# Writing the table of the first expert tiles three and four half steps later in a two-layer decoder

## Chip, core and metric

The kernel runs on one core of one Trainium2 chip. The metric is device time of one launch in microseconds (us): the median of several runs. Lower is better.

## Reference, cut to what matters

Sixteen sequences of 256 tokens with 128 features pass two decoder layers. Each layer normalises the tokens and adds, one after the other, self-attention, cross-attention to a short context, and a mixture of experts. The part that the change touches lies between layer 0's self-attention and its experts. All arithmetic is float32.

```
x = x + attn(ln(x))                       # 16 heads of 64, causal, linear bias
x = x + xattn(ln(x), ctx)                 # gate, 64 context tokens
xn = ln(x) * gamma + beta
probs = softmax(xn @ router_w); topv, topi = top_k(probs, 2)
comb = one_hot(topi) weighted by topv / sum(topv)
out = sum over e of comb[:, e] * ((silu(clip(gate_e)) * up_e) @ down_w[e])   # 8 experts
out = out + shared expert
x = x + out                               # then layer 1
```

## The kernel before, in words

**The stages.** Layer 0's self-attention goes over 16 sequences of 8 pairs of heads, 128 units. Eight chunks of 512 tokens (two sequences each) follow it: as soon as a chunk has left self-attention, its "front" (cross-attention, second normalisation, routing) is threaded between the units of later chunks. Then comes the expert stage: tokens lie in the DRAM tensor `rows_in`, sorted by expert, and 71 tiles of 128 rows (`NTILE`) are worked off one after the other; each reads its rows (`fetch`, L1315 to L1320), the gate and up weights of its expert (`weights`, L1326 to L1330) and multiplies (`hidden`, L1358 to L1369, and `down`, L1387). Layer 1 follows.

**Two tables.** Which expert a tile has, and where its rows start, is known only after the routing. The first 41 tiles (`EARLY`) are laid out as soon as six of the eight chunks are routed, so that the expert stage can start while chunks 6 and 7 are still to come; the other 30 tiles have a later table. The early table has two pieces, written in `early_pieces()`:

- the first: one matmul on TensorE that counts the routed tokens per expert (`mm_counts`, L921) and five VectorE operations on the counts (`tiles_of` and `starts_of`, L927 to L941);
- the second, `table2`: sixteen VectorE operations (`entries`, L950 to L976, then L987 to L992). L976 and L987 write `tab_a`, the row of expert numbers and the row of starting rows, that the queues read. L963 writes `etab`, used in the expert stage.

**What sets the order.** TensorE, VectorE, ScalarE and GpSimd follow a listed order in self-attention. A loop of 67 steps, two units (half steps) per step, walks the string `PLAN` and calls one piece of work per token: S scores, G the greatest of a row (L482), E exponentials (L494), R reciprocal (L502), N scaling on GpSimd (L508), T transposes (L524), C the copy of the transposes out of PSUM (L533), V the product with the values (L546), O its copy out (L556). Side pieces are entered in the dictionary `side` under a half step 2i or 2i+1; in step i, tokens m0 and m1 call their matmuls, and o0 and o1 what follows the matmul. In `PLAN`, o0 stands early and o1 late, after the last R. Each engine works strictly through its list; a piece that waits holds up all behind it on that engine.

**What the PSUM pool adds.** Transposes, the counts and the front's matmuls take turns in one PSUM pool of three buffers (`ps_m`): a transposition of a head pair needs two, and waits until an earlier user's copy has released them.

**The queues.** The expert weights (`gu`, 512 KB a tile) are issued by ScalarE between its own work, the first seven before the first expert tile; the rows (`xr`, 65 KB a tile) by SP, thirteen ahead. TensorE transposes a tile's rows (xTr, L1337), ScalarE copies them out (xTs, L1341), and the first product g (L1369) follows. Both wait for `tab_a`. SP's rows also wait for the last GpSimd scatter that fills `rows_in` (L830). Each DMA issued by ScalarE or SP signs off on one of eight DMA semaphores, shared by both and taken in turn. An issue waits until the DMA that had its semaphore before has landed, and what is behind it on the engine waits too.

Of the kernel before, what the change touches and what calls it, by code (L numbers as in the profile page):

```python
# [63 lines left out]
def kernel(ctx: ExitStack, tc: tile.TileContext, a: dict, out: bass.AP):  # L64
# [179 lines left out]
    with ExitStack() as ph:  # L244
# [669 lines left out]
        def new(what, shape):  # L914
            return fp.tile(list(shape), F32, tag=f"t_{what}", name=f"t_{what}")

        def mm_counts(tiles_seen):
            ps = tabled["ps"] = room["m"].tile(
                [P, E], F32, tag="m", name=f"counts_{tiles_seen}"
            )  # L920
            nc.tensor.matmul(ps, ones, seen[:, tiles_seen, :], start=True, stop=True)  # L921

        def tiles_of(what, less):


            cnt = new("cnt", (P, E))
            nc.vector.tensor_scalar(cnt, tabled.pop("ps"), -float(less), None, ALU.add)  # L927
            big = new("big", (P, E, T // P))
            nc.vector.tensor_tensor(
                big, cnt.unsqueeze(2).to_broadcast([P, E, T // P]), full, ALU.is_gt  # L930
            )
            num = tabled[what] = new(what, (P, E))
            nc.vector.tensor_reduce(num, big, AX.X, ALU.add)

        def starts_of(what, num):
            sq = new("sq", (P, E, E))
            nc.vector.tensor_tensor(
                sq, num.unsqueeze(1).to_broadcast([P, E, E]), lower, ALU.mult
            )
            start = tabled[what] = new(what, (P, E))  # L940
            nc.vector.tensor_reduce(start, sq, AX.X, ALU.add)  # L941

        def entries(tab, n, start, done):


            at = slice(0, EARLY) if done is None else slice(EARLY, NTILE)

            d = new("d", (1, E))
            if done is None:
                nc.vector.tensor_scalar(d, start[0:1, :], -float(P), None, ALU.mult)  # L950
            else:
                nc.vector.tensor_tensor(d, done[0:1, :], start[0:1, :], ALU.subtract)
                nc.vector.tensor_scalar(d, d, float(P), None, ALU.mult)
            dd = new("dd", (1, E))
            nc.vector.tensor_copy(dd[:, 0:1], d[:, 0:1])
            nc.vector.tensor_tensor(dd[:, 1:E], d[:, 1:E], d[:, 0 : E - 1], ALU.subtract)
            ge = new("ge", (P, EARLY, E))[:, 0:n, :]
            nc.vector.tensor_tensor(
                ge, tiles[:, 0:n, :], start.unsqueeze(1).to_broadcast([P, n, E]), ALU.is_ge
            )  # L960
            ex = new("ex", (P, EARLY))[:, 0:n]
            nc.vector.tensor_reduce(ex, ge, AX.X, ALU.add)
            nc.vector.tensor_scalar(etab[:, at], ex, -1.0, float(E + 1), ALU.mult, ALU.add)  # L963
            yield
            nc.vector.tensor_scalar(ex, ex, -1.0, None, ALU.add)
            ge, ex = ge[0:1], ex[0:1]
            nc.vector.tensor_tensor(
                ge, ge, dd.unsqueeze(1).to_broadcast([1, n, E]), ALU.mult
            )
            row = new("row", (1, EARLY))[:, 0:n]  # L970
            nc.vector.tensor_reduce(row, ge, AX.X, ALU.add)
            nc.vector.scalar_tensor_tensor(
                row, tiles[0:1, 0:n, 0], float(P), row, ALU.mult, ALU.add
            )
            nc.vector.scalar_tensor_tensor(row, ex, float(T), row, ALU.mult, ALU.add)
            nc.vector.tensor_copy(tab[:, 0, 0:n], ex)  # L976
            yield row

        def early_pieces():
            def table():  # L980
                tiles_of("num_a", P - 1)
                starts_of("start_a", tabled["num_a"])

            def table2():
                start = tabled["start_a"]
                row = list(entries(tab_a, EARLY, start, None))[-1]
                nc.vector.tensor_copy(tab_a[:, 1, :], row)  # L987

                done = tabled["done"] = new("done", (P, E))
                nc.vector.tensor_scalar(done, start, -1.0, float(EARLY), ALU.mult, ALU.add)  # L990
                nc.vector.tensor_scalar(done, done, 0.0, None, ALU.max)
                nc.vector.tensor_tensor(done, done, tabled["num_a"], ALU.min)  # L992

            return [(lambda: mm_counts(EARLY_C * TPC), table), (None, table2)]

        def late_pieces():
            def table():
                tiles_of("num_b", 0)
                left = new("left", (P, E))
                nc.vector.tensor_tensor(left, tabled["num_b"], tabled["done"], ALU.subtract)  # L1000
                starts_of("start_b", left)
                tabled["left"] = left

            def table2():
                tabled["rows"] = entries(tab_b, LATE, tabled["start_b"], tabled["done"])
                next(tabled["rows"])

            def table3():
                row = next(tabled["rows"])
                total = new("total2", (1, 1))  # L1010
                nc.vector.tensor_reduce(total, tabled["left"][0:1, :], AX.X, ALU.add)
                live = new("live", (1, LATE))
                nc.vector.tensor_scalar(live, tiles[0:1, 0:LATE, 0], total, None, ALU.is_lt)
                nc.vector.tensor_tensor(row, row, spare, ALU.subtract)
                nc.vector.tensor_tensor(row, row, live, ALU.mult)
                nc.vector.tensor_tensor(tab_b[:, 1, :], row, spare, ALU.add)

            return [(lambda: mm_counts(NT), table), (None, table2), (None, table3)]
# [8 lines left out]
        with tc.manual_schedule(engines=ordered | {mybir.EngineType.Pool}):  # L1027
# [51 lines left out]
            def plan(first, pieces):  # L1079
                for k, piece in enumerate(pieces):  # L1080
                    side.setdefault(first + k, []).append(piece)

            plan(17, [(lambda h=h: ctx_turn(h), lambda h=h: ctx_turned(h)) for h in range(2)])
            for c in range(NCHUNK):
                first_step = 16 * c + 22
                plan(first_step, front_pieces(c))
                if c == EARLY_C - 1:
                    plan(first_step + 24, early_pieces())
                if c == NCHUNK - 1:
                    plan(first_step + 25, late_pieces())  # L1090
            PLAN = (
# [35 lines left out]
            for i in range(steps // 2):  # L1127
# [13 lines left out]
                for tok, lag in plan_of:  # L1141
                    k = tok[0]
                    if k in "mo":
# [5 lines left out]
                        elif tok[1] in pieces:  # L1149
                            piece = pieces[tok[1]]  # L1150
# [405 lines left out]
    with ExitStack() as ph:  # L1556
# [230 lines left out]
        with tc.manual_schedule(engines=ordered):  # L1787
# [103 lines left out]
            plan = [w.split(":") for w in PLAN.split()]  # L1891
            plan = [(tok, int(lag)) for tok, lag in plan]
# [50 lines left out]
    with ExitStack() as ph:  # L1943
# [289 lines left out]
        plan = [part.split(":") for part in PLAN.split()]  # L2233
# [88 lines left out]
```

## Time and profile before

| | |
|---|---|
| median of 3 runs (lowest, highest) | 1412.21 us (1408.6, 1412.55) |
| the profiled execution | 1410.91 us, span 1409.0 us, mean granted TensorE clock 0.98 |
| busy share of the span: PE, DVE, ACT, POOL | 95%, 79%, 67%, 52% |
| layer 0 up to the first expert tile | 0 to 588 us: PE busy 568 us |
| expert stage | 588 to 818 us: PE busy 218 us |
| layer 1 | 818 to 1409 us: PE busy 555 us |

All further times are microseconds from the span's start. PE is TensorE's matmuls, DVE VectorE, ACT ScalarE, POOL GpSimd, SP the engine that issues most DMAs; ACTq and SPq are DMA issues. In a row of the timeline stand start, duration, engine, line, operation, output and inputs, count, and in brackets the idle time before and what ended it. The granted clock (PEclk) is a share of full speed.

### The profile page before, as it was taken

How to read it: one execution, taken by the hardware profiler on the slowest of the kernel's cores; microseconds unless marked ns; L12 is line 12 of the kernel's file. 1: busy time of each engine (PE TensorE's matmuls, PEld its weight loads, DVE VectorE, ACT ScalarE, POOL GpSimd, SP SyncE). 2: the span in 40 equal slices, each digit the busy share in tenths (PEclk: the TensorE clock that was granted, in tenths of full speed). 3: DMA queues.
4: the chain of work that ended last, by engine and by line, in shares of the span. 5: the costliest groups of instructions: out<-in, count | busy, mean ns of one | idle time of the engine just before them, and what ended most of it. 6: DMA issues, size and time to landing. Idle time of an engine off the chain costs nothing.

```text
span 1409.0 us, 37939 instructions
## 1 busy us (share of the span) xinstructions
PE 1342.1 (95%) x13205; PEld 1003.7 (71%) x13205; DVE 1108.8 (79%) x4483; ACT 942.6 (67%) x2532; POOL 733.7 (52%) x1153
## 2 busy tenths in 40 slices
PE   9999999999999999899899989999999987899998
PEld 7777777777777776689799966666666654566665
DVE  5776877777777778657779769999999977888874
ACT  6776767667676766344233349999999984776662
POOL 6463648475756656643433373553334315677751
PEclk9999999999999999999899999999999998999998
DMA  6772000000000000557577520000000000122122
GB/s 161 244 238 80 2 6 9 9 9 9 7 11 7 17 9 23 173 179 228 189 230 239 165 79 17 17 17 10 17 3 2 2 2 1 32 53 62 39 59 63
DMA packets 80349, 95.86 MB, mean 68 GB/s; under 512 B 19568, under 2 KB 62832, under 8 KB 80160
## 3 DMA queue, kind: packets, MB, share of 16 engines
q1 hardware_dynamic: 65328, 46.25, 12.0%
q10 hardware_dynamic: 10512, 38.28, 8.1%
q0 software_dynamic: 4320, 8.92, 1.9%
q8 instruction: 106, 1.74, 0.5%
q14 instruction: 83, 0.68, 0.2%
HBM read 64.24 MB, written 29.17 MB: 66 GB/s over the span
## 4 chain that ended last, share of the span: by engine, by line
PE 69%; ACT 17%; DVE 10%; issue 2%; POOL 1%; DMA 1%; POOLq 0%; ACTq 0%; SPq 0%; DVEq 0%
ACT p L1730 8%; PE pqk L414 8%; PE o L546 5%; PE s L469 5%; PE y L1387 5%; PE g L1369 5%; PE u L1369 5%; PE y L446 4%; PE t L524 4%; PE pv L431 3%; PE t L1748 3%; PE o L1772 2%; ACT pT L1759 2%; PE s L1708 2%; PE g L2149 2%
## 5 line engine op out<-in xcount | busy, mean ns | idle before, releaser
L508 POOL TENSOR_SCALAR p<-p,rs 128x128 f32<-128x128 f32 (+1 forms) x512 | 213.4, 431 | 166.3 <-DVE rs L502 124.4
L494 ACT ACTIVATE p<-p,nm 128x128 f32<-128x128 f32 (+1 forms) x512 | 226.4, 446 | 24.7 <-DVE nm L482 20.3
L1730 ACT ACTIVATE p<-p,nm 128x256 f32<-128x256 f32 x512 | 220.9, 508 | 1.7 <-DVE nm L1719 0.4
L1719 DVE CUSTOM_DVE_ANT_0 p<-s,strip 128x256 f32<-128x256 f32 x512 | 186.7, 419 | 15.3 <-PE s L1708 14.5
L533 DVE COPY pT<-t 128x384 f32<-128x384 f32 x256 | 130.2, 550 | 39.8 <-PE t L524 38.3
L482 DVE CUSTOM_DVE_ANT_0 p<-s,strip 128x128 f32<-128x128 f32 (+1 forms) x512 | 154.2, 348 | 0.5 <-PE s L469 0.2
L1397 POOL DMA_INDIRECT rows_out<-yr,to x71 | 68.5, 964 | 123.1 <-DVE yr L1396 116.3
L1748 PEld LDWEIGHTS t<-ident,p 64*128 64x128 f32 x2048 | 80.3, 140 | 54.5 <-issue 16.1
L546 PEld LDWEIGHTS o<-pT,v 128*64 128x64 f32 x1024 | 64.2, 138 | 66.4 <-issue 34.1
L425 ACT ACTIVATE k<-pqk 128x512 f32<-128x512 f32 x64 | 38.1, 596 | 108.3 <-PE pqk L414 108.3
L1748 PE MATMUL t<-ident,p 64*128 64x64 f32 x2048 | 102.9, 232 | 8.0 <-ACT pT L1759 2.4
L469 PE MATMUL s<-k,q 64*128 64x128 f32 (+1 forms) x1024 | 100.3, 332 | 0.3 <-DVE nm L482 0.3
L546 PE MATMUL o<-pT,v 128*64 128x256 f32 (+1 forms) x1024 | 99.0, 335 | 0.6 <-DVE pT L533 0.6
L1377 ACT ACTIVATE gs<-gs 128x512 f32<-128x512 f32 x71 | 44.7, 630 | 80.3 <-DVE gs L1376 62.3
L494 ACT ACTIVATION_READ_ACCUMULATOR p<-p,nm 128x1 f32 x512 | 98.0, 191 | 0.0
L524 PE MATMUL t<-ident,p 64*128 64x64 f32 x1536 | 81.6, 228 | 14.1 <-ACT pre L737 4.7
L524 PEld LDWEIGHTS t<-ident,p 64*128 64x128 f32 x1536 | 68.5, 139 | 35.7 <-POOL p L508 8.9
L1387 PE MATMUL y<-dn,hT 128*128 x568 | 79.3, 281 | 10.0 <-issue 10.0
L1708 PE MATMUL s<-k,q 32*128 32x256 f32 x1024 | 86.8, 410 | 1.4 <-DVE nm L1719 1.4
L1759 ACT COPY pT<-t 128x512 f32<-128x512 f32 x144 | 81.1, 588 | 6.8 <-PE t L1748 6.0
L440 DVE COPY v<-pv 128x512 f32<-128x512 f32 x64 | 44.2, 691 | 50.6 <-PE o L546 28.1
L1387 PEld LDWEIGHTS y<-dn,hT 128*128 128x128 f32 x568 | 71.3, 195 | 12.6 <-issue 11.8
(365 smaller groups left out, 3364.0 us busy)
## 6 DMA issues: line engine op xcount, KB each, us to landing
gu<-in_L_ffn_gate_up_w ACTq DMA_DIRECT2D x71, 512.0 KB
rows_in<-zero SPq DMA_DIRECT2D x131, 130.0 KB
spread<-wrows SPq DMA_DIRECT2D x16, 512.0 KB
xr<-rows_in SPq DMA_DIRECT2D x71, 65.0 KB
y<-rows_out SPq DMA_DIRECT2D x16, 256.0 KB
out_x<-yo SPq DMA_DIRECT2D x16, 128.0 KB
x<-in_x SPq DMA_DIRECT2D x7, 256.0 KB
rows_out<-yr,to POOLq DMA_INDIRECT x71
```

Source lines behind the costliest of these rows:

```text
L469: nc.tensor.matmul(ps_of[b, h][:, cols], q[rows, u2, iq], k[rows, u2, 0:nk], start=True, stop=True,)
L482: nc.vector.tensor_tensor_reduce(out=pr[:, cols], in0=ps[:, cols], in1=strip[:, h, P : 2 * P] if it == 0 else strip[:, h, :], scale=1.0, s ...
L494: nc.scalar.activation(pr[:, cols], pr[:, cols], AF.Exp, bias=nm[:, it : it + 1], scale=-1.0, accum_out=sm[:, it : it + 1],)
L508: nc.gpsimd.tensor_scalar(pr[:, cols], pr[:, cols], rs[:, it : it + 1], 1.0, ALU.mult, ALU.mult)
L524: nc.tensor.transpose(halves[r][:, i, blk, :], pr[rows, blk * P : (blk + 1) * P], ident[rows, rows],)
L533: nc.vector.tensor_copy(pT_of[u][:, :, :, r, :], tp_of[u][r])
L546: nc.tensor.matmul(po[rows, c0:N], v[:, jt, h % 8 * DH : (h % 8 + 1) * DH], pT[:, 0:N] if jt == 0 else pT[:, N:], start=(jt == 0), stop=(j ...
L1369: nc.tensor.matmul(ps[:, f, :], gu[:, lo + f * P : lo + (f + 1) * P], xT, start=True, stop=True,)
L1387: nc.tensor.matmul(ps, s["hT"][:, f, :], dn0[:, bass.ds(s["e"], 1), f, :].rearrange("p e d -> p (e d)"), start=(f == 0), stop=(f == NF0 - 1),)
L1719: nc.vector.tensor_tensor_reduce(out=pr[:, it, :], in0=ps[:, it, :], in1=strip1[:, h, (1 - it) * P : (1 - it) * P + N], scale=1.0, scalar= ...
L1730: nc.scalar.activation(pr[:, it, :], pr[:, it, :], AF.Exp, bias=nm[:, it : it + 1], scale=-1.0)
L1748: nc.tensor.transpose(halves[r][:, k, jt, it, :], pr[rows, it, jt * P : (jt + 1) * P], ident[rows, rows],)
```

## The change

The two pieces were planned for half steps 126 and 127 (`first_step` of chunk 5 is 102), the two halves of step 63. They go to half steps 129 and 131, the second halves of steps 64 and 65: the first piece three half steps later, the second four. No instruction is added or removed.

```
                 if c == EARLY_C - 1:
-                    plan(first_step + 24, early_pieces())
+                    for k, piece in zip((27, 29), early_pieces()):
+                        plan(first_step + k, [piece])
```

The order of the built program shows what this moves. On VectorE the five operations of the first piece stood between the pT copies (L533) of sequence 15's head pair 1 and the reciprocal L689; they now stand after the last G and R of head 13, ahead of the pT copies of pair 4. The sixteen of the second stood after the reciprocal of head 9, ahead of L701 and the pT copies of pair 2; they now stand after the last reciprocals (heads 14 and 15), ahead of L747 and the pT copies of pair 6. On TensorE the counting matmul moves from ahead of L431 to ahead of L721. On ScalarE the first seven weight issues move. They stood after the exponentials of heads 10 and 12, the copy L556 of pair 2, the exponentials of head 14, the copy of pair 4 (two issues) and the copy of pair 6. Now two stand after the copy of pair 4 and the other five after that of pair 6, all ahead of L1341, ScalarE's first work for an expert tile. SP keeps its order, but which DMA a semaphore belonged to before changes, since ScalarE's and SP's DMAs follow each other differently. GpSimd's order is the same.

## Prediction

> **What bounds the kernel.** The page first: PE is busy for 95% of the span, and the chain that ended last lies on it for 69%, DVE 10%. So a move pays where PE waits. Where it waits longest around the change is told by PE's waits between 540 and 605 us (us in total, times, longest):
>
> ```profile
> PE t L524 <- DVE rs L701: 4.2, 1, 4.2
> ```
>
> This one wait is the largest before the expert stage; the next there is 0.9. DVE's timeline tells what stood ahead of L701:
>
> ```profile
> 560.41 0.25 DVE L950 TENSOR_SCALAR t_d<-t_start_a 1x8 f32<-1x8 f32 x1
> ...
> 564.30 0.71 DVE L987 CAST tab_a<-t_row 1x41 int32<-1x41 f32 x1
> ...
> 565.63 0.17 DVE L701 RECIPROCAL rs<-sm 128x4 f32<-128x4 f32 x1
> ```
>
> The reader is to see the second piece, L950 to L992, hold DVE from 560.41 to L701's start: 5.2 us. PE had the PSUM buffer that L701 releases to wait for. Stretches of that time show what came after (us, then PE, PEld, DVE, ACT, POOL busy, granted clock, DMA):
>
> ```profile
> 561.80:565.90 4.10, 0.00 (x0) 0.00 (x0) 3.85 (x14) 0.73 (x4) 3.68 (x7) 0.91 0.10 32
> 566.00:572.00 6.00, 5.98 (x39) 4.41 (x40) 4.56 (x25) 2.56 (x9) 3.58 (x6) 0.50 0.67 197
> ```
>
> PE stood still, and then ran six microseconds at half clock. Last, ACT's timeline before the first expert tile:
>
> ```profile
> 579.92 4.16 ACTq L1330 DMA_DIRECT2D gu<-in_L_ffn_gate_up_w  x2
> 584.12 0.58 ACT L556 COPY oT<-o 128x512 f32<-128x512 f32 x1 [4.34 <-DMA xr<-rows_in]
> 584.86 0.36 ACTq L1330 DMA_DIRECT2D gu<-in_L_ffn_gate_up_w  x1
> 588.22 0.81 ACT L1341 ACTIVATE xTs<-xTr,bet,gam 128x128 f32<-128x128 f32 x2 [3.51 <-PE xTr L1337]
> ```
>
> Two weight issues spread over 4.16 us: the second waited until row tile 4 had landed, and the copy behind it waited too. xTs, on which the first expert product waits, starts at 588.22 because PE was late.
>
> **What goes.** The first piece held DVE from 556.29 (L927) to 557.79 (L689): 1.5 us that everything behind it on DVE and ACT saw. The second goes too; L701 then follows at about 559.1, when PE's sums (L695, 0.6 us after 558.5) are done. PE need no longer wait: transposes of pair 2 end at 559.5, scores (1.53) at 561.0, and pair 3's transposes start there, not at 565.95: 4.9 us earlier. If PE keeps its clock, they and their followers run at the times of undisturbed rows: 12 transposes 0.58 for 1.25, L708 0.66 for 1.12, L546 0.87 a pair for 2.77 in two; the L721 and L728 pairs 1.7 each. They end at 567.5 where they ended at 574.78. **Lead: 7.2 us.**
>
> **What comes back.** The first piece lies in DVE's idle 5.4 us before the pT copies of pair 4, which wait for ACT's two tanh (L737) anyway: nothing; without that cover 1.6 us. These copies end at 570.8 (before 578.2), two reciprocals at 571.0, and there the second piece now starts: 5.3 us in which the pT copies of pair 6, ready at 572.4, wait. Then L747 (0.67). Copies 576.9, pair 7's transposes 577.5 (they need a buffer that those copies free), last product 580.1, output product L446 (4.06) 584.2, its addition 584.6, xTr 585.1. Before, the second xTr ended at 588.2. **PE's side leads by 3.1.** But PE now idles from 572.4 to 577.5, 5.1 us, longer than the 4.18 that halved its clock. At half clock for the same 6.8 us, 3.4 us of PE work are lost less what waits anyway: about 2.7, xTr at 587.8. From nothing lost to 2.7: lead 3.1 or 0.4.
>
> **The new wait.** ACT and SP read the table when L987 is done: 4.6 us after the second piece's start, so 575.6 instead of 565.02. SP's first row issue was released by the last scatter then, at 575.80, long after the table; the scatters now land by 571 (last issue near 566.5, 3.8 us as before). The table now comes last, and SP needs 1.7 us from it to the issue (565.04 to 566.7 in its records): 577.3. Each further row tile takes 1.14 (thirteen table loads from 576.2 to 589.9), so row tile 7 is issued at 585.3. On ACT, weights 0 and 1 go out at 576 and 577, the copy of pair 6 at 580.1, weight 2 at 581.4. Counting each DMA semaphore's users in the built program, weight 3 waits for row tile 1, weight 4 for 3, **weight 5 for 6 and weight 6 for 7**; before, the last two waited for 4 and 6. xTs stands behind weight 6. Behind xTs stand the table load and the silu, and DVE, PE and the next tile wait for these.
>
> How long row tile 7 takes to land, the trace's packet records bound: of the first ten row tiles, from issue to the last receipt, tile 6 took 1.5 us, tile 8, issued amid weights, 4.0; the ten average 2.7, and tiles 7 and 9, also amid weights, took 3.5. Weights 1 to 4 are on the move here, so I take 3.1, between these two. Tile 7 lands at 588.4, weight 6 is out 0.4 later, and xTs starts at **588.9**; with 1.5 at 587.3, with 4.0 at 589.8. Weight 5 (tile 6: issued 584.1, landing 587.2, the next issue 1.1 after) asks for no more. PE's side, 585.1 or 587.8, is earlier. **Sum: 588.9 - 588.2 = +0.7 us**, with ends -0.9 and +1.6.
>
> In the expert stage the weights come later but not too late: seven tiles of 512 KB and thirteen of 65 KB from 577 on, at the 258 GB/s moved in 585 to 590, are there by 595; the seventh is wanted at about 609 (the first product of tile 6 started at 608.2). Cost nothing; at 139 GB/s (590 to 595) they would come at 610, and the cover is gone. PE is busy for 218 of that stage's 230 us, so a late start is carried to the end. Layer 1 has the same order and costs.
>
> [...] The row: 4.18 us idle, then 0.50 granted; waits of 0.6 us and less between 572 and 600 left it at 1.00. [...]
>
> **Rivals.**
> 1. **Slower: half clock at the first tiles.** Place: PE waits for xTs with xTr done. It decides from an idle between 0.6 us (kept) and 4.18 (halved); mine is 3.8 if the clock held before, 1.1 if not. Price: 6.8 us at half clock lose up to 3.4, less DVE and ACT waits in the first tiles (PE busy 4.8 to 5.0 of 5 there): 2 to 3.4. With the +0.7: +2.7 to +4.1, with the ends +1.6 to +5; 1414.5. For it: the idle is real in my sum. Against: the first idle probably takes the drop.
> 2. **Faster: the queues don't bite.** Row tiles land sooner than in 1.5 us of their issue, or SP issues them faster than every 1.14; then PE's side decides: -0.9 to -3.1, middle 1408.9. For it: 3.1 us of lead stand on PE. Against: ACT's 4.34 us wait of before is the same mechanism.
> 3. **Slower: weights late.** If the burst moves at 139 to 150 GB/s, tiles 3 to 6 wait 0.5 to 1 us each on top of rival 1: +4.3 to +8, 1417.
> 4. **Faster: the lead stays.** The second piece overlaps PE's products more than I think: -4.3 to -7.2 (the whole lead), 1405.
> 5. That the change doesn't do what it says: the listed order shows it does; no case of its own.
>
> **How the numbers follow.** The profiled execution took 1410.91, 1.91 around its span and 1.3 below the median 1412.21; I sum against it. Forecast 1410.91 + 0.7 = **1411.6**, its own range 1410.0 to 1412.5 (-0.9 to +1.6): 0.42. Rival 1 0.20, rival 2 0.16, rival 3 0.14, rival 4 0.08. About 0.3%, 4.2 us, is what a measurement of this kernel can tell from no change. Faster by more: rival 4 and a sliver of 2, 0.10. Slower by more: rival 3 and 0.06 of rival 1, 0.20. Same: 0.70. Leaving out rival 4 and the upper part of 3, the range goes from 1407.3 (-3.1, and 0.5 for the spread of the runs) to 1417.2 (+5, and 1.3 for profile against median).
>
> **What would show it.** Right: DVE's L950 begins near 571 with no PE wait on L701; PE idles some 5 us before pair 7's transposes; SP's first row issue at 577, right after the table; ACT's wait "DMA xr" stretching over weights 3 to 6, xTs near 589 with PE's xTr long done. Wrong: xTs right behind PE's xTr at 585 to 586 (rival 2), half clock after 589 (rival 1), first products waiting for gu (rival 3), or pT copies of pair 6 not held up (rival 4).

## Result and profile after

The changed kernel takes 1413.65 us (median of 22 runs, 1410.39 to 1417.18), the kernel before, run beside it as often, 1410.47 us (1406.51 to 1413.81). The ratio is 1.0026, 95% interval 1.0018 to 1.0035: **slower by about 3.7 us** (2.5 to 4.9). A second set (experiment 5) gave 1.0027 (1.0012 to 1.0041). The forecast was +0.7 us. The measured time lies inside its range and within the 0.3% that it called no change, but it is a real loss, five times the size of the one summed. The profiled execution took 1412.53 us with a span of 1410.7, so this one profile shows +1.6; single executions of either kernel scatter by 7 us, and the medians are the measure.

The waits of PE between 540 and 605 us, after (us in total, times, longest):

```profile
PE g L1370 <- DMA xr<-rows_in: 6.1, 1, 6.1
PE t L524 <- DVE pT L533: 4.0, 1, 4.0
PE t L524 <- POOL p L508: 1.4, 3, 1.0
```

The wait for L701 has gone, as forecast. Two others, 4.0 and 6.1 us, stand where one of 4.2 stood: the first is that for the pT copies of pair 6, the second ends at the first expert product. DVE's timeline shows the second piece at its new place (start, duration, engine, line, operation):

```profile
558.80 0.16 DVE L701 RECIPROCAL rs<-sm 128x4 f32<-128x4 f32 x1
...
570.08 0.41 DVE L950 TENSOR_SCALAR t_d<-t_start_a 1x8 f32<-1x8 f32 x1
...
573.65 1.98 DVE L975 SCALAR_TENSOR_TENSOR t_row<-t_ex,t_row 1x41 f32<-1x41 f32 x1
...
575.66 0.17 DVE L987 CAST tab_a<-t_row 1x41 int32<-1x41 f32 x1
...
576.84 1.02 DVE L533 COPY pT<-t 128x384 f32<-128x384 f32 x2
```

L701 runs at 558.80 and no longer at 565.63. The second piece holds DVE from 570.08, the table is written at 575.8, and the pT copies of pair 6 follow at 576.84. What ACT and PE did before the first expert tile, from their two timelines:

```profile
581.15 0.59 ACT L556 COPY oT<-o 128x512 f32<-128x512 f32 x1 [9.56 <-PE o L546]
581.87 9.76 ACTq L1331 DMA_DIRECT2D gu<-in_L_ffn_gate_up_w  x5
591.76 0.81 ACT L1342 ACTIVATE xTs<-xTr,bet,gam 128x128 f32<-128x128 f32 x2 [10.03 <-POOL vpad L1274]
```

```profile
585.76 0.44 PE L1338 MATMUL xTr<-ident,xr 128*128 128x128 f32 x2 [0.52 <-DVE x L454]
592.27 2.07 PE L1370 MATMUL g<-xTs,gu 128*128 128x128 f32 x8 [6.08 <-DMA xr<-rows_in]
```

Five weight issues spread over 9.76 us: they start at 581.87, 583.09, 584.21, 590.15 and 591.28, and the gap is weight 5 waiting for row tile 6. xTs stands behind them, at 591.76, with PE's xTr done since 586.2. (The releaser put to ACT's idle, POOL's vpad, ended at 591.59, but xTs doesn't read it: the two met by chance. In the second run of this kernel the same row names "DMA xr<-rows_in".) The same stretches as before, and three more (us, then PE, PEld, DVE, ACT, POOL busy, granted clock, DMA share, GB/s):

```profile
561.80:565.90 4.10, 3.80 (x24) 2.39 (x24) 3.85 (x23) 1.45 (x5) 3.74 (x6) 1.00 0.10 32
566.00:572.00 6.00, 3.72 (x46) 2.33 (x46) 3.90 (x12) 3.41 (x11) 5.76 (x9) 1.00 0.09 25
...
577.00:582.00 5.00, 4.55 (x32) 3.35 (x33) 3.31 (x9) 0.59 (x1) 0.00 (x0) 0.51 0.76 234
586.50:592.20 5.70, 0.00 (x0) 0.00 (x0) 0.00 (x0) 0.43 (x2) 5.09 (x9) 0.69 0.77 223
588.70:595.50 6.80, 3.23 (x15) 3.23 (x16) 1.08 (x4) 2.48 (x4) 2.89 (x9) 0.50 0.74 224
```

PE works where it stood still before (561.8 to 565.9) at full clock, but stands still from 586.5 to 592.2, and both new idles halve its clock: 0.51 after the first, 0.50 over the first two expert tiles.

### The profile page after: what moved, and what is told of

It is laid out like the page before. It is cut to its first block, busy times and chain, and to the rows that moved or that the text cites. A ratio compares the mean times of both kernels' runs of the same rounds, so it can differ in the third digit from the quotient of the medians.

```text
span 1410.7 us, 37935 instructions
## 1 busy us (share of the span) xinstructions
PE 1335.5 (95%) x13205; PEld 999.8 (71%) x13205; DVE 1109.3 (79%) x4483; ACT 943.3 (67%) x2532; POOL 735.9 (52%) x1153
## 4 chain that ended last, share of the span: by engine, by line
PE 68%; ACT 16%; DVE 10%; issue 2%; POOL 1%; DMA 1%; another core or an unknown queue 1%; SPq 1%; POOLq 0%; ACTq 0%; DVEq 0%
ACT p L1731 8%; PE pqk L414 8%; PE s L469 5%; PE o L546 5%; PE g L1370 4%; PE u L1370 4%; PE y L1388 4%; PE y L446 4%; PE t L524 4%; PE pv L431 3%; PE t L1749 3%; PE o L1773 2%; PE s L1709 2%; ACT pT L1760 2%; PE g L2150 2%
## 5 line engine op out<-in xcount | busy, mean ns | idle before, releaser
L508 POOL TENSOR_SCALAR p<-p,rs 128x128 f32<-128x128 f32 (+1 forms) x512 | 214.9, 435 | 161.1 <-DVE rs L502 119.6
L533 DVE COPY pT<-t 128x384 f32<-128x384 f32 x256 | 130.4, 550 | 36.9 <-PE t L524 35.1
L1370 PE MATMUL g<-xTs,gu 128*128 128x128 f32 x568 | 78.1, 282 | 14.3 <-ACT xTs L1342 8.1
L1370 PEld LDWEIGHTS g<-xTs,gu 128*128 128x128 f32 x568 | 71.4, 197 | 16.1 <-ACT xTs L1342 15.1
```

The lines of the kernel that those rows point to most:

```text
L508: nc.gpsimd.tensor_scalar(pr[:, cols], pr[:, cols], rs[:, it : it + 1], 1.0, ALU.mult, ALU.mult)
L533: nc.vector.tensor_copy(pT_of[u][:, :, :, r, :], tp_of[u][r])
L1370: nc.tensor.matmul(ps[:, f, :], gu[:, lo + f * P : lo + (f + 1) * P], xT, start=True, stop=True,)
```

## The experiments

**Theory:** the start of the expert stage is set by ACT's queue. Weights 5 and 6 wait for row tiles 6 and 7, these land late because weights are on the move at the same time, xTs stands behind the issues, and the half clock that follows PE's idle adds about 1 us. **Rivals:** the half clock, or weights and transfers that come late, are the loss; or DVE's hold of pair 6 is.

The sets ran on different chips: the kernel before took 1398.3, 1410.1 and 1399.4 us in the three sets below, so that times are compared as ratios to the kernel before in the same set. The changed kernel itself ran beside experiments 6 to 8, not beside 1 to 4, 9 and 10; for those its ratio is from another set. Up to the first expert tiles the profiles of all chips can be laid on each other to about a microsecond and a half: the transposes of pair 4 start at 567.26 and 567.41 in the changed kernel's two and at 566.72 in experiment 1, and xTr in experiment 2 starts 1.56 us ahead of the kernel before, whose stretch of half clock was longer (6.83 and not 3.41 us).

**1 and 2: xTs ahead of the late issues, in the changed kernel and in the one before.**

```
-            for i in range(AHEAD - 1):
+            for i in range(5):
                 weights(i)
...
                 if i < NTILE:
                     gated(i)
+                if i == 0:
+                    for j in range(5, AHEAD - 1):
+                        weights(j)
```

> The changed kernel with one more edit: before the expert stage only weights 0 to 4 are issued, and weights 5 and 6 behind the first tile's silu, so that the first xTs no longer stands behind the two issues that wait for row tiles 6 and 7. Theory A (ACT's queue behind the late row tiles sets the start of the expert stage): xTs starts right behind PE's xTr, near 586.5 instead of 591.8, PE's idle shrinks from 6.1 to about 1 us, no half clock at the first tiles, and the time is some 5 us below the changed kernel's, 1408 to 1410, that is 0.5 to 3.5 us below the kernel before. Theory B (the half clock and the late transfers of weights cost the time, the start of xTs does not): the first tiles wait for weights instead, and the time stays 2.5 to 4 us above the kernel before.

> The same edit of the weight issues in the kernel before. Theory A: there xTs waited for PE and not for ACT's queue, so nothing is to be had: within 0.7 us of the kernel before. If the edit by itself is worth several us (rival: late weight issues help the row tiles and the other traffic whatever the table does), it shows here too, and the first experiment says nothing about the changed kernel's loss.

Measured: 1.0004 (0.9984 to 1.0025) and 1.0008 (0.9992 to 1.0024) of the kernel before, medians 1399.56 and 1399.54 us. PE's timeline of the first:

```profile
586.75 1.13 PE L1370 MATMUL g<-xTs,gu 128*128 128x128 f32 x8 [0.58 <-DMA xr<-rows_in]
...
594.41 1.16 PE L1370 MATMUL g<-xTs,gu 128*128 128x128 f32 x8 [3.64 <-ACT xTs L1342]
```

and ACT's:

```profile
590.82 2.97 ACTq L1331 DMA_DIRECT2D gu<-in_L_ffn_gate_up_w  x3
593.90 0.46 ACT L1342 ACTIVATE xTs<-xTr,bet,gam 128x128 f32<-128x128 f32 x1 [4.63 <-DMA gu<-in_L_ffn_gate_up_w]
```

xTs starts at 586.18, right behind xTr, and the first products run at full clock (1.00 from 585 to 590): 5.6 us of theory A came as said. The time came back by 3, not 5 us, because the issues now hold up a later xTs: the products of the third tile wait 3.64 us. The kernel before pays for the edit in the same place (2.18 us there), within its uncertainty. What matters: **with xTs out of the queue on both sides, the move of the pieces costs nothing that can be told from zero** (medians 0.02 us apart; the scatter of the runs allows some 3 us either way, so this pair alone doesn't rule out most of the 3.7).

**3: PE kept busy in its second idle.**

```
+                if i == 0:
+                    spin = ps_m.tile([P, P], F32, tag="m", name="spin")
+                    for _ in range(22):
+                        nc.tensor.matmul(spin, ones, ones, start=True, stop=True)
                 if i < NTILE:
                     hidden(i)
```

> The changed kernel with 22 products of ones by ones on PE between the first xTr transposes and the first expert product, some 4.8 us that lie in PE's 6.1 us idle; nothing reads them. Theory A (the start counts most, the half clock adds about 1 us): xTs stays near 591.8, the clock stays at 1.00 behind it, and the time is 0.9 to 1.6 us below the changed kernel's, still 1.5 to 3 us above the kernel before. Theory B (the half clock is the loss): nearly all of the 3.5 us comes back. If the clock is not what the idle costs, nothing changes.

Measured: 1.0017 (1.0001 to 1.0034), against 1.0026 of the changed kernel: about 1.3 us less, though the intervals overlap. PE's first product and one stretch:

```profile
592.05 1.16 PE L1370 MATMUL g<-xTs,gu 128*128 128x128 f32 x8 [0.55 <-ACT xTs L1342]
```

```profile
590.00:595.00 5.00, 4.45 (x40) 4.26 (x39) 1.65 (x7) 2.72 (x4) 2.13 (x6) 1.00 0.73 229
```

xTs stays where it was (591.54), the clock holds at 1.00, the first product takes 1.16 and not 2.07 us. As far as overlapping intervals can tell, the half clock is a part of the loss, about a third or less, and the late start is the rest.

**4: only the second piece moved.**

```
-                    for k, piece in zip((27, 29), early_pieces()):
+                    for k, piece in zip((24, 29), early_pieces()):
```

> Only the second piece is moved (five steps later than in the kernel before), the first stays where the kernel before has it. By my steps the first piece holds DVE for 1.5 us ahead of L701 again, and the second starts and ends about 1.3 us later: table near 577, first row tile issued near 578.6, xTs near 593, 1 to 1.5 us above the changed kernel. Rival: the first piece costs nothing in either place, since the later DVE idle takes up what it delays: within 0.5 us of the changed kernel.

Measured: 1.0044 (1.0023 to 1.0064), some 2.5 us above the changed kernel. The first row issue came 1.35 us later (578.78), xTs 1.13 (592.89), as reckoned; xTr 2.1 (587.85):

```profile
593.40 2.07 PE L1370 MATMUL g<-xTs,gu 128*128 128x128 f32 x8 [5.12 <-ACT xTs L1342]
```

That the first piece's later place is worth its 1.5 us fits the profile; the interval (3.2 to 8.9 us above the kernel before) overlaps the changed kernel's and doesn't show it by itself.

**5 and 6: the changed kernel again, and with small weights.**

```
+            few = 256 if i in (2, 3, 4) else 2 * F0
             nc.scalar.dma_start(
-                gu, a["L0_ffn_gate_up_w"][bass.ds(e, 1)].rearrange("e d f -> d (e f)")
+                gu[:, 0:few],
+                a["L0_ffn_gate_up_w"][bass.ds(e, 1)].rearrange("e d f -> d (e f)")[:, 0:few],
             )
...
-                        ps[:, f, :], gu[:, lo + f * P : lo + (f + 1) * P], xT,
+                        ps[:, f, :], gu[:, at(lo + f * P) : at(lo + f * P) + P], xT,
```

Here `at` takes a column modulo 256 in tiles 2, 3 and 4, so that this kernel leaves out a part of the computation.

> The changed kernel itself once more, beside the others of this set and as often as they. [...]

> The changed kernel, in which weights 2, 3 and 4 fetch 256 of their 1024 columns (128 KB in place of 512) and the products of these three tiles read those columns four times over: that part of the computation is left out, the instructions of the engines are the same. The fewer packets also change which transfers share a completion semaphore: weight 5 now waits for row tile 3 and weight 6 for row tile 5. Theory A (row tiles are late because weights are on the move in the same engines, and ACT's queue hands that on): row tiles 5 to 7 land 2 to 3 us after their issue in place of 3.9 to 4.6, the last weight is issued near 586.5, xTs starts at 586.8 to 587.5 right behind xTr, there is no half clock behind it, and 4 to 5 us of the changed kernel's time go, to 0.5 to 2 us below the kernel before. Theory B (SP's own issues make row tiles late): rows 5 to 7 still take 4 us. Theory C (the start of the first tile is not what costs): the time stays.

Measured: 1.0027 (1.0012 to 1.0041) and **0.9990** (0.9979 to 1.0001): 5 us between them. In the traces a row tile's issue is followed by sixteen updates of its semaphore (tile 6 of the changed kernel: 588.89 to 590.13), and the issue that waits for it goes out behind the last (weight 5: 590.15); so the last is taken as the landing. From the traces' semaphore records, microseconds from a row tile's issue to that update:

```
row tile                      3     4     5     6     7
before                      2.75  3.34  2.38  1.82  3.85
changed                     2.59  3.57  5.14  5.87  4.94
changed, second run         3.06  4.14  4.51  3.86  4.81
small weights 2, 3 and 4    2.50  2.29  2.56  2.64  4.65
```

(The prediction counted completion packets over all DMA engines in order of time instead. That gives up to 1.3 us less in this table, 4.62 for tile 6 of the changed kernel, since a tile's updates are spread and late ones come behind early ones of the next: tile 7's first there came at 589.13, a microsecond ahead of tile 6's last.) With small weights on the move, row tiles 4 to 6 land in 2.3 to 2.6 us; tile 7, issued beside the next large weight, takes 4.65 again. SP issued all of them at the same moments as in the changed kernel (tile 6 at 584.26 in both), so theory B of this expectation is out. ACT and PE of the kernel with small weights:

```profile
581.88 4.74 ACTq L1332 DMA_DIRECT2D gu<-in_L_ffn_gate_up_w  x5
586.75 0.81 ACT L1344 ACTIVATE xTs<-xTr,bet,gam 128x128 f32<-128x128 f32 x2 [5.01 <-DMA gu<-in_L_ffn_gate_up_w]
```

```profile
587.26 1.16 PE L1372 MATMUL g<-xTs,gu 128*128 128x128 f32 x8 [0.97 <-ACT xTs L1344]
```

Five issues take 4.74 us and not 9.76, and xTs follows 5 us sooner. This run doesn't part the fewer bytes from the other partners on the semaphores: weights 5 and 6 have tiles 3 and 5 before them there, and tile 7, which landed only at 590.04, holds up nothing on ACT. That the queue hands the delay on is shown by the semaphores of the changed kernel (tile 6's last update at 590.13, weight 5 at 590.15) and by the first experiment's profile; that large weights on the move make the delay, by the table.

**7 and 8: the pieces in between.** The pairs are (26, 27); the eighth has the edit of the first as well.

```
-                    for k, piece in zip((27, 29), early_pieces()):
+                    for k, piece in zip((26, 27), early_pieces()):
```

> Both pieces between the kernel before and the changed one: the first at step +26, ahead of L715, the second at +27, right behind the reciprocals of head 13 and ahead of the pT copies of pair 4, where DVE idled for 3.6 us. Expected: second piece 565.7 to 571, no wait of PE for L701, pT copies of pair 4 held by about 3 us but those of pair 6 no longer; table ready near 570.5, first row tile issued near 572, row tile 7 landing by 584; xTr near 583, xTs at 584 to 586, 2 to 4 us ahead of the kernel before. Theory A: 1 to 4 us below the kernel before. Rival: a wait of the same length as the one before now stands ahead of pair 4, PE's clock is halved there as well, and the time is that of the kernel before within 1 us.

> The same places of the pieces, and weights 5 and 6 issued behind the first tile's silu. If ACT's queue still holds xTs at the new place, xTs comes up to 2 us earlier than without this edit and the time falls as much; if the row tiles are early enough, the edit only makes weights 5 and 6 late and costs 0.5 to 1.5 us, as it seems to in the kernel before.

Measured: **0.9989** (0.9979 to 1.0000) and 0.9992 (0.9983 to 1.0000): 1.1 to 1.6 us below the kernel before, at the edge of what can be told, and 5 us below the changed one. PE's waits in the seventh, and its ACT:

```profile
PE t L524 <- DVE pT L533: 4.9, 2, 4.4
PE g L1370 <- ACT xTs L1342: 1.0, 1, 1.0
```

```profile
577.32 2.78 ACTq L1331 DMA_DIRECT2D gu<-in_L_ffn_gate_up_w  x2
580.59 0.59 ACT L556 COPY oT<-o 128x512 f32<-128x512 f32 x1 [3.41 <-PE o L546]
581.44 4.17 ACTq L1331 DMA_DIRECT2D gu<-in_L_ffn_gate_up_w  x3
585.74 0.81 ACT L1342 ACTIVATE xTs<-xTr,bet,gam 128x128 f32<-128x128 f32 x2 [4.56 <-DMA gu<-in_L_ffn_gate_up_w]
```

PE still waits 4.4 us for DVE, about as long as before (4.2) and as in the changed kernel (4.0), and is halved behind it (0.53 granted from 573 to 578). But the table stands at 571.5, the row tiles are 4 us earlier, and xTs is ready within 0.5 us of xTr. So a DVE hold of this length doesn't decide; what is behind the table does. The edit of the first experiment adds nothing here, as expected once the rows are early.

**9 and 10: the second piece cut in two.** Its first six instructions go ahead of the pT copies of pair 4; the tenth has the edit of the first as well.

```
+            def table2a():
+                tabled["half"] = entries(tab_a, EARLY, tabled["start_a"], None)
+                next(tabled["half"])
+
-            def table2():
+            def table2b():
                 start = tabled["start_a"]
-                row = list(entries(tab_a, EARLY, start, None))[-1]
+                row = list(tabled.pop("half"))[-1]
...
-                    for k, piece in zip((27, 29), early_pieces()):
+                    for k, piece in zip((27, 27, 29), early_pieces()):
```

> The changed kernel with the second piece cut in two: its first six instructions (L950 to L963, 2.1 us) go to step +27 behind the first piece, into the 3.6 us that DVE idles ahead of the pT copies of pair 4, and only the rest (L965 to L992) stays at step +29. Expected: the rest runs from 570.1 to about 573, just as the pT copies of pair 6 become ready, so that PE's 4.0 us wait and the half clock behind it go; table near 572.7 (1.8 more if one of its operations is stretched again), first row tile issued near 574.3, xTr at 580 to 582. The completion semaphores are shared as in the changed kernel, so by theory A xTs still stands behind weights 5 and 6, which wait for row tiles 6 and 7: rows issued at 581.1 and 582.2 land by 585 to 586.5, xTs starts at 586.5 to 588.5, PE idles 5 us or more and may lose its clock: between 2.5 us below and 1 us above the kernel before. Rival (PE's own wait ahead of pair 7 was the loss): xTs follows xTr at 581 to 583 and 5 to 7 us are gained.

> The same cut, and weights 5 and 6 issued behind the first tile's silu. Theory A: xTs starts right behind xTr, at 580.5 to 582.5, 6 to 8 us ahead of the kernel before; some of it is lost at tile 3, where xTs waits behind the late weights (2 to 4 us, as in the two kernels before with this edit), so 2 to 6 us below the kernel before. Rival: the first tiles wait for their weights and row tiles instead, and it is no better than the kernel with the cut alone.

Measured: 1.0008 (0.9991 to 1.0025) and 0.9994 (0.9976 to 1.0011). The queue did what theory A says (xTs 587.90 with the issues ahead of it, 585.38 without), but PE's wait ahead of pair 7 only shrank to 3.3 us and xTr came at 585, not at 580 to 582: the rest of the piece took to 575.4. DVE and POOL of the ninth:

```profile
573.40 1.99 DVE L996 TENSOR_TENSOR t_done<-t_done,t_num_a 128x8 f32<-128x8 f32 x1
575.31 0.68 DVE L747 SCALAR_TENSOR_TENSOR xn<-pre,xn 128x512 f32<-128x512 f32 x1
```

```profile
574.11 1.25 POOL L750 TENSOR_TENSOR x<-x,pre 128x512 f32<-128x512 f32 x1
```

An operation on 128x8, 0.17 us in the changed kernel (L992), took 1.99 here and ended with POOL's L750 (575.36). More of this below. As a better version the cut is not settled: its intervals reach both sides of the kernel before.

**All together.** Column one is the start of xTs, two the shift of the silu of the ninth expert tile against the profile before, three the ratio less one, times the set's time of the kernel before:

```
                         xTs      shift    measured, us
before                  588.22      0           0
changed                 591.76    +4.4        +3.7
changed, second run     590.90    +3.6        +3.8
1 changed, xTs ahead    586.18    +1.8        +0.6
2 before, xTs ahead     586.66    +0.7        +1.1
3 PE kept busy          591.54    +3.3        +2.4
4 second piece only     592.89    +5.5        +6.2
6 small weights         586.75    -1.5        -1.4
7 at 26 and 27          585.74    -2.5        -1.6
8 the same, xTs ahead   585.19    -2.3        -1.1
9 cut in two            587.90    +0.4        +1.1
10 the same, xTs ahead  585.38    -1.3        -0.8
```

The shift at the ninth tile, of one profile each, tells the measured time within 1.3 us throughout: to that accuracy, what the change does is done by then.

## Why the prediction was wrong

**What goes** was right: L701 at 558.80 (559.1), no wait behind it, the products of pre ended at 566.6 (567.5), the first piece ran inside DVE's idle.

**What comes back** was right: the second piece began at 570.08 (571.0), held pair 6 to 576.84 (576.9), the clock was halved from 575.0 to 581.85, and xTr ended at 586.2, between the 585.1 and 587.8 given. That the piece's end was met is luck and hides two misses: it began 0.9 earlier and lasted 6.2, not 5.3 us. PE's idle was 4.0 and not 5.1 us, as waits for POOL's scaling (1.4 in all) came ahead of it.

**The new wait** was right up to the issue: table 575.8 (575.6), first row issue 577.43 (577.3), row tile 7 issued at 585.39 (585.3), every 1.13.

**The step that failed** is the size of one term, the landing: "I take 3.1, between these two. Tile 7 lands at 588.4, weight 6 is out 0.4 later, and xTs starts at 588.9", together with "Weight 5 (tile 6: issued 584.1, landing 587.2, the next issue 1.1 after) asks for no more". Tile 6 took 5.87 us and tile 7 4.94. Weight 5 went out at 590.15, 0.02 behind tile 6's last update; weight 6 followed 1.13 later, with tile 7 landed at 590.33, and xTs started at 591.76. (In the second run the two took 3.86 and 4.81, weight 6 went out at 590.41, 0.02 behind tile 7's last update, and xTs started at 590.90.) So xTs was 3.5 us later than before, in the second run 2.7, and not 0.7.

Even the upper bound of the prediction, "4.0" from tile 8 of before, gave only 589.8, because that row was misread: by the semaphores tile 8 took 5.27 us, tile 6 1.82, and the ten tiles average 3.5, not 2.7. With 5.3 in the same sum xTs starts at 591.1, +2.9 us. So a row of before did bound the term; the count of packets had made it too small, and the choice of the middle did the rest. Experiment 6 measures the term for tiles 4 to 6 both ways: 2.3 to 2.6 us without three large weights on the move, 3.6 to 5.9 with them.

**The clock.** Experiment 3 puts the price of the second half clock at about 1 us. Rival 1 (slower, 1414.5) comes nearest to the measured time, but by luck: it charged 2 to 3.4 us to the half clock and 0.7 to the late xTs, and measured were about 1 and 2.7 to 3.5. I weighed against it that "the first idle probably takes the drop": both idles took one, at 575.02 and 588.68, 1.6 and 2.5 us after PE's last work. The halved stretches were 6.83 us each; behind the same first idle they were 10.24 in experiments 3 and 4. No run shows what sets their length.

**The rest** held: no product of the first tiles waited for its weights in the changed kernel (rival 3; none of PE's waits there names gu); rival 4 didn't come. Rival 2's price is seen where its condition is made: with early rows the start came 1.5 to 2.5 us ahead of before (experiments 6 and 7).

Open: how much of the row tiles' delay is the weights' bytes and how much the number of packets ahead, and why single tiles of the same kernel differ by up to two microseconds between runs (5.87 and 3.86 for tile 6).

## To carry to other kernels

A transfer's landing time is to be taken from a row under the load it will meet, and from the updates of its own semaphore: here small transfers landed after 2.3 to 2.6 us without three large loads on the move and after 3.6 to 5.9 with them, and a count of packets read 4.0 where the semaphore says 5.3. Where DMAs of two engines take turns on a few completion semaphores, look up which issue waits for which transfer, and put nothing urgent on the issuing engine behind those. A freed wait is worth only what the next gate leaves: here 8 us of lead on PE (the transposes of pair 4 at 567.26 and not at 575.46) had shrunk to 2 at xTr, and ended in a queue that had been hidden by 3 us (weight 6 out at 585.2, xTs at 588.22).

## What the hardware showed that was not expected

Some DVE operations stretched from 0.2 to 2 us, and each ended within 0.13 us of the end of a POOL operation on two tensors: L975 in the changed kernel (1.98 us, ended 575.63, POOL's L750 575.57), L972 in experiment 7 (1.79 us, ended 570.62, POOL's L742 570.50), L996 in experiment 9 (1.99 us, 575.39 and 575.36). L975 took 1.97 us in experiment 5 and 1.98 in experiment 6. POOL in the changed kernel:

```profile
574.32 1.25 POOL L750 TENSOR_TENSOR x<-x,pre 128x512 f32<-128x512 f32 x1
```

Copies out of PSUM kept their 0.55 us beside such an operation (two of L533 from 569.01 in the changed kernel, 0.55 and 0.56, beside POOL's L742, 569.11 to 570.39). That the DVE operation waits for POOL's to end is the author's reading of the coinciding ends. The rows agree in part: the stretched operations started 0.4 to 0.7 us ahead of the POOL operation with which they ended, and L972, also of two inputs, took its 0.21 us at 573.40 in the changed kernel while POOL scaled (L508). No run here moved POOL's operation away, so that it is the cause is argued, not shown. The stretch (1.98 us for L975's 0.19 before) put the table 1.8 us later in the changed kernel; before, the second piece had met only POOL's shorter operations (L508, two in 0.82 to 1.16 us, and the scatters L830, 1.04 to 1.17).
